# Layer 0 of a graph stack: seven block products in place of eight, and batch norm stepped block by block

## The chip, the cores and the metric

The kernel runs on one core of one Trainium2 chip, as one launch, all in float32. The metric is device time in microseconds (us). The times given for the kernel before are the median and the spread of three runs; the profile is of one further execution.

Names used below: PE is TensorE, ACT is ScalarE, DVE is VectorE, POOL is GpSimd, SP is SyncE, whose queue carries most transfers.

## What is computed

The reference is a stack of four graph layers over 128 graphs of 64 nodes and 256 features. Only layer 0 is touched by the change:

```python
h = jnp.maximum(_layernorm(x, axis=-1), 0.0)
agg = jnp.einsum('nm,bmd->bnd', A_hat, h)           # A_hat: normalized adjacency, 64 x 64
x1 = agg.reshape(-1, 256)
h = relu(_batchnorm(x1 @ W1.T + b1, g1, be1))       # W1: 512 x 256
out = _batchnorm(h @ W2.T + b2, g2, be2)            # W2: 256 x 512
x = x + out.reshape(128, 64, 256)
```

`_batchnorm` takes mean and variance over all 8192 rows, so nothing after the first product can be finished before the first product of every row is done, and the same holds for the second. Layers 1 to 3 (two graph convolutions with four LSTMs over windows, a masked attention, a four-head attention) follow; of them only the LSTM's bias, `bih + bhh`, is touched.

## The kernel before

The 8192 rows are cut into `NCH` = 16 chunks of `CH` = 512 rows. Results lie channels on partitions: one chunk of the first product is 4 blocks of 128 channels x 512 rows (`KH` = 4), its input 2 blocks (`KD` = 2).

**First stage, lines 452 to 521.** Per chunk: `norm0` (line 345) loads x on SP's queue, takes the layer norm's moments on DVE (lines 159, 160), the inverse root and the shift on POOL (lines 99, 100, 182, 183) and applies norm and relu in four tiles on ACT (line 187). `aggregate0` (line 349) multiplies by the adjacency in 64 small matmuls on PE (line 214) and copies the two PSUM banks, one by DVE (line 354), one by ACT (line 356). `product1` (line 358) is the product with W1: for each of four blocks two matmuls of 128x128 weights with 512 columns (line 369), an ACT copy that adds the bias (line 371), and DVE's batch-norm statistics (line 372). For chunks 1 to 15 only PE's order is that of the program (line 495); the order on the other engines is the planner's. On PE the order is aggregate of chunk c+1, product of chunk c.

**Batch norm, line 515.** `bn_params` (line 286) handles block after block: DVE aggregates the statistics (line 295), POOL takes the inverse root, three small DVE operations make scale and shift. `relu2` (line 375) applies them to chunks 0 and 1, and `product2` (line 521, matmuls on line 385) starts the second product on these two.

**Second stage, lines 591 to 659.** For chunks 2 to 14 the second product is already done by seven products of blocks (`Seven2`, line 398) in place of eight: input and weights are cut in two by two, four sums of input blocks (`differences`, line 304) and four sums of weights (`w2_sums`, made on POOL at line 508) are formed, and seven products (line 432) are combined through three PSUM banks X, Y and Z, with copies on ACT (line 439) and additions on DVE (line 443). All engines but SP follow the program's order. Chunk 15 comes last, by the plain product (lines 662 to 667), followed by the second batch norm and the first convolutions of layer 1 (the order list `START`).

What follows in the change uses the same scheme. The pool `l0b` has two buffers under the tag `h1`, `l0` two each under `h` and `agg` and three under `xt`; PSUM has eight banks. A tile that takes over a buffer waits for the last use of the tile that had it.

Of the kernel before, what the change touches and what calls it, by code (L numbers as in the profile page):

```python
# [8 lines left out]
F32 = mybir.dt.float32  # L9
AF = mybir.ActivationFunctionType  # L10
# [9 lines left out]
def kernel(  # L20
# [265 lines left out]
    def bn_params(stats, bn, pool, name, biased):  # L286


        n = stats.shape[1]
        mv = pool.tile([P, n, 2], F32, name=f"mv_{name}")  # L290
        sc = pool.tile([P, n], F32, name=f"sc_{name}")
        sh = pool.tile([P, n], F32, name=f"sh_{name}")
        for m in range(n):
            one = slice(m, m + 1)
            nc.vector.bn_aggr(mv[:, m, :], stats[:, m, :, :].rearrange("p c s -> p (c s)"))
            rsqrt(sc[:, one], mv[:, m, 1:2], EPS)
            if not biased:
                nc.vector.tensor_add(mv[:, m, 0:1], mv[:, m, 0:1], bn[:, 0, one])
            nc.vector.tensor_mul(sc[:, one], sc[:, one], bn[:, 1, one])
            nc.vector.tensor_mul(sh[:, one], mv[:, m, 0:1], sc[:, one])  # L300
            nc.vector.tensor_sub(sh[:, one], bn[:, 2, one], sh[:, one])
        return sc, sh
# [35 lines left out]

    def load0(c):
        xt = l0.tile([P, NJ, D], F32, tag="xt", name=f"xt_{c}", bufs=3)  # L340
        nc.sync.dma_start(xt, xr[c])
        hs[c] = l0.tile([P, NJ, D], F32, tag="h", name=f"h_{c}")
        return xt

    def norm0(c):
        xt = load0(c)
        ln_apply(hs[c], xt, *ln_stats(xt, f"a{c}"), f"a{c}", by_pool=True)

    def aggregate0(c):
        aggs[c] = l0.tile([P, KD, CH], F32, tag="agg", name=f"agg_{c}")  # L350
        dst = aggs[c].rearrange("p k (j e t) -> p e (k j) t", e=2, t=T)
        for e, ps in enumerate(aggregate(hs.pop(c), ahat_t, f"a{c}")):
            if e == 0:
                nc.vector.tensor_copy(dst[:, e], ps)
            else:
                nc.scalar.copy(dst[:, e], ps)

    def product1(c):
        agg = aggs.pop(c)
# [3 lines left out]
        for m in range(KH):  # L363
            if c == 0 and 2 * m == KH:
                aggregate0(1)
                ln_apply(hs[2], *third, "a2")
            ps = bank(f"z1_{c}_{m}")
            for k in range(KD):
                nc.tensor.matmul(ps, w1_sb[:, k, m * P : (m + 1) * P], agg[:, k, :],  # L369
                                 start=(k == 0), stop=(k == KD - 1))  # L370
            nc.scalar.activation(z1[c][m], ps, AF.Identity, bias=bn1_sb[:, 0, m : m + 1])
            nc.vector.bn_stats(st1[:, m, c, :], z1[c][m])
        z2[c], z1whole[c] = lo, (lo, hi)
# [15 lines left out]
    def result2(c, m, ps):  # L389
        nc.vector.tensor_scalar(z2[c][:, m, :], ps, bn2_sb[:, 0, m : m + 1], None, op0=OP.add)  # L390
# [7 lines left out]
    class Seven2:  # L398
# [39 lines left out]
        def copy(self, m, j, tag):  # L438
            nc.scalar.activation(self.part(m, j), self.banks[tag], AF.Identity,
                                 bias=bn2_sb[:, 0, m : m + 1])  # L440
# [6 lines left out]

    halves2 = [slice(0, CH // 2), slice(CH // 2, CH)]
# [3 lines left out]
    with tc.manual_schedule(engines={mybir.EngineType.PE, mybir.EngineType.DVE,  # L452
# [6 lines left out]
        xts = [l0.tile([P, NJ, D], F32, tag="xt", name=f"xt_{c}", bufs=3) for c in range(2)]  # L459
# [31 lines left out]
        xt = load0(2)  # L491
        third = xt, *ln_stats(xt, "a2")
        product1(0)
    tc.no_sync_barrier()
    with tc.manual_schedule(engines={mybir.EngineType.PE}):
# [5 lines left out]
        nc.gpsimd.dma_start(w2_sb, w2t.rearrange("(k p) f -> p k f", p=P))  # L501
        w2_sums = l0b.tile([P, 4, KH // 2, P], F32, name="w2_sums", bufs=1)
        a = w2_sb.rearrange("p (i k) (m f) -> p i m k f", i=2, m=KD)
        for dst, u, v, op in ((0, a[:, 0, 1], a[:, 1, 1], OP.add),
                              (1, w2_sums[:, 0], a[:, 0, 0], OP.subtract),
                              (2, a[:, 0, 0], a[:, 0, 1], OP.subtract),
                              (3, a[:, 1, 0], w2_sums[:, 1], OP.subtract)):
            nc.gpsimd.tensor_tensor(w2_sums[:, dst], u, v, op)
        for c in range(1, NCH):
            if c + 1 < NCH:  # L510
                aggregate0(c + 1)
            if c + 2 < NCH:
                norm0(c + 2)
            product1(c)
        sc1, sh1 = bn_params(st1, bn1_sb, w0, "bn1", True)
        for c in range(2):
            new_h1(c)
        for k in range(KH):
            for c in range(2):
                relu2(c, k)  # L520
# [140 lines left out]
    with tc.manual_schedule(engines={mybir.EngineType.PE}):  # L661
        c = NCH - 1
        banks = product2([c], False)
        for m in range(KD):
            result2(c, m, banks[c, m])
            stats2(c, m)
        sc2, sh2 = bn_params(st2, bn2_sb, const, "bn2", True)
# [19 lines left out]
    nc.vector.tensor_add(bias, bias, bias2)  # L687
# [503 lines left out]
    with tc.manual_schedule(engines={mybir.EngineType.PE, mybir.EngineType.DVE, mybir.EngineType.Pool,  # L1191
# [5 lines left out]
        for n, i in enumerate(START):  # L1197
            if n == 5:
                nc.vector.tensor_add(c2, c2_ps[:, :D], bg1_sb)
            for at, fill, name in ((6, 16, "d"), (9, 6, "e"), (10, 6, "f")):  # L1200
# [573 lines left out]
```

## Time and profile before

| what | value |
|---|---|
| median of three runs | 1912.3 us (1910.05 to 1912.66) |
| the profiled execution | 1910.73 us |
| its span, first to last instruction | 1908.6 us |
| PE, DVE, ACT, POOL busy in the span | 99%, 62%, 51%, 23% |
| granted TensorE clock | 1.0 |
| first product of chunks 1 to 15 | 23.4 to 144.4 us of the span |
| second product, all chunks | 144.4 to 246.8 us of the span |

How to read it: times in the views are from the start of the span. A row of the groups view has the line, the engine, the operation, output<-input, shape and count, then busy time and the mean of one instruction, then the idle time ahead of it and what ended it. Instructions of ACT, DVE and POOL that follow each other without a wait overlap a little: the distance from start to start is shorter than the duration. A float32 matmul shows as two records.

### The profile page before, as it was taken

Reading aid. Unit: us, or ns where it says so; the run is one execution under the profiler, and the core shown is the slowest. Engines: PE = TensorE matmul, PEld = TensorE weight load, DVE = VectorE, ACT = ScalarE, POOL = GpSimd, SP = SyncE. Lnnn points to the kernel's source line nnn. Section 1 sums busy time; section 2 is a strip of 40 time slices with the busy share of each in tenths; the row PEclk is TensorE's granted clock in tenths of the full one; section 3 lists DMA queues with packets and bytes.
Section 4 is the critical chain, followed back from the end, with each engine's and each line's share of the span. In section 5 each row is a group of like instructions: output and inputs, shape, how many; then the busy total and the mean of one; then the engine's idle time right before and its main releaser. Section 6 shows DMA issues by size and latency. Waiting matters only on the chain.

```text
span 1908.6 us, 38821 instructions
## 1 busy us (share of the span) xinstructions
PE 1887.0 (99%) x15137; PEld 1488.3 (78%) x15137; DVE 1190.7 (62%) x3070; ACT 979.5 (51%) x2184; POOL 444.6 (23%) x632
## 2 busy tenths in 40 slices
PE   8999999999999999999999999999999999999998
PEld 5446866886897898799689789879969967777776
DVE  6647844556557656655755764665555567777776
ACT  5657734455456455455544645545554544444453
POOL 4205711211211211121121121112112213232332
PEclk9999999999999999999999999999999999999999
DMA  4113653115424522531632452352144245444433
GB/s 137 60 39 138 223 195 108 49 78 188 132 84 161 182 84 77 189 103 70 215 117 84 161 182 84 103 186 100 54 155 127 92 133 156 134 150 139 144 112 112
DMA packets 110502, 240.39 MB, mean 126 GB/s; under 512 B 11376, under 2 KB 74352, under 8 KB 110320
## 3 DMA queue, kind: packets, MB, share of 16 engines
q1 hardware_dynamic: 109568, 236.57, 37.1%
q8 instruction: 120, 1.97, 0.4%
q0 software_dynamic: 320, 1.05, 0.2%
q14 instruction: 62, 0.51, 0.1%
q10 hardware_dynamic: 432, 0.30, 0.1%
HBM read 169.98 MB, written 67.90 MB: 125 GB/s over the span
## 4 chain that ended last, share of the span: by engine, by line
PE 93%; DVE 4%; ACT 1%; issue 1%; POOL 1%; DMA 0%; SPq 0%; DVEq 0%; ACTq 0%; POOLq 0%
PE x L990 23%; PE g L954 18%; PE z L990 11%; PE y L990 6%; PE v L1264 6%; PE z L369 5%; PE p_q L1271 3%; PE u L743 3%; PE v L729 3%; PE X L1460 3%; PE X L432 2%; PE Y L1460 1%; PE z L385 1%; PE Y L432 1%; PE agg_c L214 1%; PE o L1587 1%
## 5 line engine op out<-in xcount | busy, mean ns | idle before, releaser
L999 DVE TENSOR_TENSOR gates<-gates,x 128x128 f32<-128x128 f32 (+2 forms) x384 | 119.4, 322 | 333.1 <-PE x L990 327.7
L990 PE MATMUL x<-xd,wset 128*128 128x128 f32 (+2 forms) x1280 | 285.0, 310 | 0.1
L990 PE MATMUL x<-hd,wset 128*128 128x128 f32 (+2 forms) x1152 | 246.7, 303 | 0.0
L1048 POOL TENSOR_TENSOR gates<-gates 128x512 f32<-128x512 f32 (+2 forms) x48 | 75.0, 1562 | 647.9 <-ACT gates L882 647.9
L990 PEld LDWEIGHTS x<-xd,wset 128*128 128x128 f32 x1280 | 202.1, 190 | 16.9 <-DVE gates L999 3.1
L882 ACT ACTIVATE gates<-gates,bias 128x256 f32<-128x256 f32 (+4 forms) x384 | 170.4, 490 | 66.4 <-DVE gates L999 63.6
L990 PEld LDWEIGHTS x<-hd,wset 128*128 128x128 f32 x1152 | 185.1, 191 | 5.0
L933 ACT ACTIVATE gates<-g,bias 128x512 f32<-128x512 f32 (+2 forms) x240 | 138.2, 610 | 97.7 <-PE g L954 94.4
L954 PE MATMUL g<-hT,wset 128*128 128x256 f32 (+2 forms) x744 | 184.4, 405 | 1.1 <-DVE hT L893 1.1
L954 PEld LDWEIGHTS g<-hT,wset 128*128 128x128 f32 x744 | 140.5, 190 | 44.1 <-issue 8.8
L954 PE MATMUL g<-hT,wih 128*128 128x512 f32 x384 | 166.4, 592 | 0.0
L996 ACT COPY gates<-y 128x128 f32<-128x128 f32 (+2 forms) x192 | 54.2, 294 | 204.8 <-PE y L990 204.3
L990 PE MATMUL z<-hs,wset 128*128 128x128 f32 (+2 forms) x768 | 154.1, 303 | 0.0
L954 PEld LDWEIGHTS g<-hT,wih 128*128 128x128 f32 x384 | 72.3, 190 | 87.7 <-issue 83.0
L990 PEld LDWEIGHTS z<-hs,wset 128*128 128x128 f32 x768 | 119.8, 191 | 3.3
L369 PE MATMUL z<-agg,w_sb 128*128 128x512 f32 x256 | 114.1, 598 | 0.0
L939 DVE TENSOR_TENSOR cell<-gates 128x512 f32<-128x512 f32 (+2 forms) x80 | 50.5, 650 | 101.6 <-ACT gates L933 101.5
L999 DVE TENSOR_TENSOR gates<-gates,z 128x128 f32<-128x128 f32 (+2 forms) x384 | 104.6, 316 | 0.2
L996 ACT COPY gates<-x 128x128 f32<-128x128 f32 (+2 forms) x192 | 56.5, 296 | 93.7 <-PE x L990 93.0
L882 ACT ACTIVATE gates<-x,bias 128x128 f32<-128x128 f32 (+2 forms) x192 | 74.8, 390 | 50.9 <-PE x L990 48.1
L990 PE MATMUL z<-hT,wset 128*128 128x128 f32 (+1 forms) x512 | 96.9, 301 | 0.0
L369 PEld LDWEIGHTS z<-agg,w_sb 128*128 128x128 f32 x256 | 47.3, 190 | 54.6 <-issue 51.4
(271 smaller groups left out, 3827.0 us busy)
## 6 DMA issues: line engine op xcount, KB each, us to landing
wset<-wfar SPq DMA_DIRECT2D x96, 960.0 KB, 6.4
hT<-far_h SPq DMA_DIRECT2D x124, 128.0 KB, 2.9
far_h<-hm SPq DMA_DIRECT2D x16, 512.0 KB, 3.0
far_n<-xs SPq DMA_DIRECT2D x16, 512.0 KB, 6.9
xs<-far_n SPq DMA_DIRECT2D x64, 128.0 KB, 3.1
far_x<-xs SPq DMA_DIRECT2D x16, 512.0 KB, 3.0
x<-far_x SPq DMA_DIRECT2D x64, 128.0 KB, 3.2
xt<-in_x_dram SPq DMA_DIRECT2D x15, 512.0 KB, 4.0
```

The source lines that it names most:

```text
L369: nc.tensor.matmul(ps, w1_sb[:, k, m * P : (m + 1) * P], agg[:, k, :], start=(k == 0), stop=(k == KD - 1))
L432: nc.tensor.matmul(self.banks[tag], w, right[:, k, :], start=first and not k, stop=True, skip_group_check=True)
L729: nc.tensor.matmul(banks[m], wg0_sb[:, k, m * P : (m + 1) * P], agg[:, k, :], start=(k == 0), stop=(k == KD - 1))
L882: nc.scalar.activation(gate(q, c, part), src, AF.Tanh if q == 2 else AF.Sigmoid, bias=bs[:, q * KD + c : q * KD + c + 1])
L933: nc.scalar.activation(columns_of(gate(q, c)), natural(banks[q, c][:, :n].rearrange("p (w b) -> p w b", b=nb)), AF.Tanh if q == 2 else AF. ...
L954: nc.tensor.matmul(banks[q, c][:, :n].rearrange("p (w b) -> p w b", b=nb)[:, w, :], block(q, c, k), hv[:, k, w.start * p : (w.stop - 1) * ...
L990: nc.tensor.matmul(folded(self.psum(kind)), wsets[p, self.q][:, BLOCKS[kind][i], :], (ox[self.s] if part == "x" else oh)[kind], start=firs ...
L996: nc.scalar.copy(gate(self.q, kind // 5, halves[kind // 5]), self.psum(kind))
L999: nc.vector.tensor_add(gate(self.q, *dst), gate(self.q, *a), self.psum(kind))
L1048: nc.gpsimd.tensor_mul(gates[:, 0, :, :n], gates[:, 0, :, :n], gates[:, 2, :, :n])
L1264: nc.tensor.matmul(ps[:, i, :], hT[:, k, j, :], w[:, k, first : first + D], start=(k == 0), stop=(k == KD - 1))
L1460: nc.tensor.matmul(st[c, tag][:, i * CH // 2 : (i + 1) * CH // 2].rearrange("p (a n) -> p a n", n=P), w, st[c, "o7"][kind], start=first an ...
```

## The change

The first product of chunks 2 to 14 is done by seven block products (`Seven1`). The input chunk is cut in two blocks of channels times two halves of 256 rows; the sums of input blocks are formed on POOL per chunk (`differences`, 4 operations of 128x256), those of weights once (`w1_sums`, 4 operations). Each product is two matmul pairs of 256 columns into the halves of a bank. Products 7 and 4 of a chunk are done during the next chunk's turn. The addition of Z to block (0, 0) is done on POOL (`c11`), from an SBUF copy of Z made by ACT; the other two additions are on DVE. The four engines PE, DVE, ACT and POOL now follow a written order in this stage. Both PSUM banks of the aggregate are copied by ACT there. `w2_sums` moves from the stage's head into turns 7 to 10.

Biases of the two products are no longer added to the results; `bn_steps` adds the bias to the mean and gives it back in the shift, in two more small DVE operations per block. `bn_steps` is a generator: for the first batch norm its two halves for each block, and the relus of chunks 0 and 1, stand between the blocks of chunk 15. For the second, DVE takes chunk 15's statistics from PSUM, and ACT copies the result. `bias + bias2` for the LSTM is added a little later, at the fifth step of `START`.

```diff
-    def bn_params(stats, bn, pool, name, biased):
...
             one = slice(m, m + 1)
             nc.vector.bn_aggr(mv[:, m, :], stats[:, m, :, :].rearrange("p c s -> p (c s)"))
             rsqrt(sc[:, one], mv[:, m, 1:2], EPS)
+            yield
             if not biased:
                 nc.vector.tensor_add(mv[:, m, 0:1], mv[:, m, 0:1], bn[:, 0, one])
             nc.vector.tensor_mul(sc[:, one], sc[:, one], bn[:, 1, one])
             nc.vector.tensor_mul(sh[:, one], mv[:, m, 0:1], sc[:, one])
             nc.vector.tensor_sub(sh[:, one], bn[:, 2, one], sh[:, one])
-        return sc, sh
+            if not biased:
+                nc.vector.scalar_tensor_tensor(sh[:, one], bn[:, 0, one], sc[:, one], sh[:, one],
+                                               op0=OP.mult, op1=OP.add)
+            yield sc, sh
...
     def load0(c):
+            xts[c] = l0.tile([P, NJ, D], F32, tag="xt", name=f"xt_{c}", bufs=3)
+            nc.sync.dma_start(xts[c], xr[c])
...
+    def moments0(c):
+        return ln_moments(xts[c], f"a{c}", range(NJ)) if c < NCH else iter(())
+    def shift0(c, late):
+        for mv, rstd in late:
+            nmr = small.tile([P, NJ], F32, tag=f"ln_nmr{NJ}", name=f"nmr_a{c}")
+            nc.gpsimd.tensor_tensor(nmr, mv[:, :, 0], rstd, OP.mult)
+            nc.gpsimd.tensor_scalar(nmr, nmr, -1.0, None, op0=OP.mult)
+            shifts[c] = rstd, nmr
+    def apply0(c, *tiles):
...
+        for j in tiles:
+            nc.scalar.activation(hs[c][:, j, :], xts[c][:, j, :], AF.Relu, bias=nmr[:, j : j + 1],
+                                 scale=rstd[:, j : j + 1])
+    def aggregate0(c, by_both=True):
         aggs[c] = l0.tile([P, KD, CH], F32, tag="agg", name=f"agg_{c}")
         dst = aggs[c].rearrange("p k (j e t) -> p e (k j) t", e=2, t=T)
         for e, ps in enumerate(aggregate(hs.pop(c), ahat_t, f"a{c}")):
-            if e == 0:
+            if by_both and e == 0:
                 nc.vector.tensor_copy(dst[:, e], ps)
             else:
                 nc.scalar.copy(dst[:, e], ps)
-    def product1(c):
...
-            ps = bank(f"z1_{c}_{m}")
-            for k in range(KD):
-                nc.tensor.matmul(ps, w1_sb[:, k, m * P : (m + 1) * P], agg[:, k, :],
-                                 start=(k == 0), stop=(k == KD - 1))
-            nc.scalar.activation(z1[c][m], ps, AF.Identity, bias=bn1_sb[:, 0, m : m + 1])
+    def stats1(c, *ms):
+        for m in ms:
             nc.vector.bn_stats(st1[:, m, c, :], z1[c][m])
...
+    def block1(c, m, agg):
+        ps = bank(f"z1_{c}_{m}")
+        for k in range(KD):
+            nc.tensor.matmul(ps, w1_sb[:, k, m * P : (m + 1) * P], agg[:, k, :], start=(k == 0),
+                             stop=(k == KD - 1))
+        nc.scalar.copy(z1[c][m], ps)
+    class Seven1:
...
+        def __init__(self, c):
+            self.c, self.banks = c, {}
+            agg = aggs.pop(c)
+            b = {(k, j): agg[:, k, halves2[j]] for k in range(KD) for j in range(2)}
+            t = l0b.tile([P, KH, CH], F32, tag="h1", name=f"t1_{c}").rearrange("p k n -> p (k n)")
+            n = CH // 2
+            self.z = t[:, 4 * n : 6 * n]
+            t = [t[:, i * n : (i + 1) * n] for i in range(4)]
+            self.sums = differences(nc.gpsimd, t, b[0, 0], b[0, 1], b[1, 0], b[1, 1])
+            self.at = {1: b[0, 0], 2: b[1, 0], 3: b[1, 1], 4: t[3], 5: t[0], 6: t[1], 7: t[2]}
+        def product(self, kind, tag):
+            first = tag not in self.banks
+            if first:
+                self.banks[tag] = bank(f"{tag}1_{self.c}")
+            for i in range(2):
+                if kind in (1, 2, 4):
+                    m, k = {1: (0, 0), 2: (0, 1), 4: (1, 1)}[kind]
+                    w = w1_sb[:, k, (2 * m + i) * P : (2 * m + i + 1) * P]
+                else:
+                    w = w1_sums[:, {5: 0, 6: 1, 7: 2, 3: 3}[kind], i * P : (i + 1) * P]
+                nc.tensor.matmul(self.banks[tag][:, i * CH // 2 : (i + 1) * CH // 2], w, self.at[kind],
+                                 start=first and not i, stop=True, skip_group_check=True)
...
+        def copy(self, m, j, tag):
+            nc.scalar.copy(self.part(m, j), self.ps(tag))
+        def add(self, m, j, tag):
+            nc.vector.tensor_add(self.part(m, j), self.part(m, j), self.ps(tag))
+        def c11(self):
+            nc.gpsimd.tensor_tensor(self.part(0, 0), self.part(0, 0),
+                                    self.z.rearrange("p (i n) -> p i n", i=2), OP.add)
...
     def result2(c, m, ps):
-        nc.vector.tensor_scalar(z2[c][:, m, :], ps, bn2_sb[:, 0, m : m + 1], None, op0=OP.add)
+        nc.vector.tensor_copy(z2[c][:, m, :], ps)
...
         def copy(self, m, j, tag):
-            nc.scalar.activation(self.part(m, j), self.banks[tag], AF.Identity,
-                                 bias=bn2_sb[:, 0, m : m + 1])
+            nc.scalar.copy(self.part(m, j), self.banks[tag])
...
         l0b, close_l0b = pool("l0b", 2, "right")
         w2_sb = l0b.tile([P, KH, D], F32, name="w2_sb", bufs=1)
         nc.gpsimd.dma_start(w2_sb, w2t.rearrange("(k p) f -> p k f", p=P))
+        w1_sums = l0.tile([P, 4, D], F32, name="w1_sums", bufs=1)
         w2_sums = l0b.tile([P, 4, KH // 2, P], F32, name="w2_sums", bufs=1)
-        a = w2_sb.rearrange("p (i k) (m f) -> p i m k f", i=2, m=KD)
-        for dst, u, v, op in ((0, a[:, 0, 1], a[:, 1, 1], OP.add),
-                              (1, w2_sums[:, 0], a[:, 0, 0], OP.subtract),
...
-            nc.gpsimd.tensor_tensor(w2_sums[:, dst], u, v, op)
-        for c in range(1, NCH):
-            if c + 1 < NCH:
-                aggregate0(c + 1)
-            if c + 2 < NCH:
-                norm0(c + 2)
-            product1(c)
-        sc1, sh1 = bn_params(st1, bn1_sb, w0, "bn1", True)
-        for c in range(2):
-            new_h1(c)
-        for k in range(KH):
-            for c in range(2):
-                relu2(c, k)
+    def sums_of(dst, a):
+        return [lambda d=d, u=u, v=v, op=op: nc.gpsimd.tensor_tensor(dst[:, d], u, v, op)
+                for d, u, v, op in ((0, a[:, 0, 1], a[:, 1, 1], OP.add),
+                                    (1, dst[:, 0], a[:, 0, 0], OP.subtract),
+                                    (2, a[:, 0, 0], a[:, 0, 1], OP.subtract),
+                                    (3, a[:, 1, 0], dst[:, 1], OP.subtract))]
...
+    with tc.manual_schedule(engines={mybir.EngineType.PE, mybir.EngineType.DVE,
+                                     mybir.EngineType.Activation, mybir.EngineType.Pool}):
+        load0(3)
+        load0(4)
+        aggregate0(2)
+        late = moments0(3)
+        for _ in range(NJ):
+            next(late)
+        shift0(3, late)
+        for f in sums_of(w1_sums, w1_sb.rearrange("p k (m f) -> p k m f", m=2)):
+            f()
+        late = moments0(4)
+        next(late)
+        sevens = {2: Seven1(2)}
+        new_z1(1)
+        agg = aggs.pop(1)
+        load0(5)
+        for m in range(KH):
+            block1(1, m, agg)
+            if m < NJ - 1:
+                next(late)
+                apply0(3, *((0, 1), (2,), (3,))[m])
+            if m == NJ - 2:
+                shift0(4, late)
+            stats1(1, m)
+        for f in sevens[2].sums:
+            f()
+        more = sums_of(w2_sums, w2_sb.rearrange("p (i k) (m f) -> p i m k f", i=2, m=KD))
+        for c in range(2, NCH - 1):
+            a, z = sevens[c], sevens.get(c - 1)
+            new_z1(c)
+            load0(c + 4)
+            aggregate0(c + 1, False)
+            b = sevens[c + 1] = Seven1(c + 1) if c + 1 < NCH - 1 else None
+            late = moments0(c + 3)
+            a.product(2, "Z")
+            nc.scalar.copy(a.z, a.banks["Z"])
+            next(late, None)
+            next(late, None)
+            if z:
+                z.product(7, "X")
+                z.add(1, 1, "X")
+            if b:
+                for f in b.sums:
+                    f()
+            a.product(1, "X")
+            a.copy(0, 0, "X")
+            apply0(c + 2, 0)
+            a.c11()
+            if z:
+                stats1(c - 1, 0, 1)
+            a.product(5, "Y")
+            a.copy(1, 1, "Y")
+            apply0(c + 2, 1)
+            next(late, None)
+            next(late, None)
+            if z:
+                z.product(4, "X")
+                z.copy(1, 0, "X")
+            apply0(c + 2, 2)
+            shift0(c + 3, late)
+            if c > 6 and more:
+                more.pop(0)()
+            if z:
+                stats1(c - 1, 2, 3)
+            a.product(6, "X")
+            a.copy(0, 1, "X")
+            apply0(c + 2, 3)
+            a.product(3, "Y")
+            a.add(0, 1, "Y")
+        c = NCH - 1
+        new_z1(c)
+        agg = aggs.pop(c)
+        for m in range(KH):
+            if not m:
+                a.product(7, "X")
+                a.add(1, 1, "X")
+                stats1(c - 1, 0, 1)
+            if m == 1:
+                a.product(4, "X")
+                a.copy(1, 0, "X")
+                stats1(c - 1, 2, 3)
+            block1(c, m, agg)
+            stats1(c, m)
+            if not m:
+                steps1 = bn_steps(st1, bn1_sb, w0, "bn1", False)
+            else:
+                sc1, sh1 = next(steps1)
+                if m == 1:
+                    for i in range(2):
+                        new_h1(i)
+                for i in range(2):
+                    relu2(i, m - 1)
+            next(steps1)
+        sc1, sh1 = next(steps1)
+        for i in range(2):
+            relu2(i, m)
...
         banks = product2([0, 1], True)
...
         c = NCH - 1
         banks = product2([c], False)
         for m in range(KD):
-            result2(c, m, banks[c, m])
-            stats2(c, m)
-        sc2, sh2 = bn_params(st2, bn2_sb, const, "bn2", True)
+            nc.vector.bn_stats(st2[:, m, c, :], banks[c, m])
+            nc.scalar.copy(z2[c][:, m, :], banks[c, m])
+        *_, (sc2, sh2) = bn_steps(st2, bn2_sb, const, "bn2", False)
         c2_ps = weight_products()
...
-    nc.vector.tensor_add(bias, bias, bias2)
...
         for n, i in enumerate(START):
             if n == 5:
                 nc.vector.tensor_add(c2, c2_ps[:, :D], bg1_sb)
+                nc.vector.tensor_add(bias, bias, bias2)
```

## The prediction

> **What bounds the kernel now.** I read the page's busy shares first, then the chain that ended last, then the busy times of the stage that the change rewrites.
>
> ```profile
> PE 1887.0 (99%) x15137; PEld 1488.3 (78%) x15137; DVE 1190.7 (62%) x3070; ACT 979.5 (51%) x2184; POOL 444.6 (23%) x632
> ```
>
> PE is the bound over the whole span. The chain of waits, in order of time, shows the first stage (first two lines: one chunk) and a product of the second stage:
>
> ```profile
> 40.88 7.06 PE z L369 x16
> 47.95 1.09 PE agg_a L214 x64
> ...
> 186.10 1.73 PE X L432 x8
> ```
>
> A chunk costs PE 7.06 + 1.09 = 8.15 us in the first stage, and nothing else is on the chain. The stretch that holds chunks 2 to 14 (columns: length, then busy time of PE, PEld, DVE, ACT, POOL):
>
> ```profile
> 30.57:137.30 106.73, 106.42 (x1040) 52.22 (x1041) 60.83 (x153) 67.66 (x118) 20.52 (x48) 1.00 0.20 64
> ```
>
> PE has 0.3 us idle here, ACT 39, DVE 46, POOL 86. So less PE work pays directly, until one of the three is in the way.
>
> **What PE saves.** Two products of four records take 1.73 us in the chain, one 0.8635. Seven take 6.04 us where the plain product takes 7.06; with the aggregate a chunk needs 7.13. That is 1.02 us x 13 = 13.3 us. With it goes the wait at the first aggregate of the loop: in PE's timeline chunk 3's aggregate takes 1.94 us and 0.22 ahead of it, against 1.16, since its relus were late; about 0.9. If PE never waited, it would be at the second product 14.1 us earlier.
>
> **What the helpers now do per chunk.** Start-to-start distances are taken from ACT's and POOL's timelines:
>
> ```profile
> 33.75 1.58 ACT L187 ACTIVATE h<-xt,nmr_a,rstd_a 128x256 f32<-128x256 f32 x3
> 35.23 0.57 ACT L356 COPY agg<-agg_a 128x512 f32<-128x512 f32 x1
> 35.74 0.60 ACT L187 ACTIVATE h<-xt,nmr_a,rstd_a 128x256 f32<-128x256 f32 x1
> ```
>
> ```profile
> 25.17 1.41 POOL L508 TENSOR_TENSOR w_sums<-w_sb 128x256 f32<-128x256 f32 x2 [3.67 <-DMA w_sb<-in_w2t_dram]
> ...
> 195.79 3.70 POOL L580 TENSOR_TENSOR ws<-ws 128x256 f32<-128x256 f32 x4
> ...
> 235.27 2.91 POOL L580 TENSOR_TENSOR ws<-ws 128x256 f32<-128x256 f32 x4 [3.18 <-DMA ws<-in_whh_t_dram]
> ```
>
> ACT: a relu tile every 0.49 us, a copy of 512 every 0.48 (0.57 to 0.59 alone). New per chunk: seven copies and four relus, 5.3 us of 7.13. DVE: four moment pairs at 0.53 (starts 16.20, 16.76 in its timeline), four statistics at 0.60, two PSUM additions at 0.60: 5.7. POOL: inverse root and shift 1.98 with gaps (starts 91.41 to 93.37), four sums, `c11`. Nearest rows for the sums: 0.70 each undisturbed (1.41 for two), 0.93 beside DVE (3.70 for four); for `c11`, 128x512: 1.27 (row L1048) to 1.78 (the slow instances of L309). The Trainium skill (SBUF — State Buffer, section "Who interferes with whom") says that a DVE instruction with at most one SBUF input does not hold GpSimd up. The 3.70 ran beside DVE's L310 and L311 (two SBUF inputs), the 2.91 beside statistics and PSUM additions, and the new stage has only the latter kinds. By the page and that row I take 2.88 for the sums and 1.35 for `c11`, gaps included; by the disturbed rows they would be 3.8 and 1.86. POOL: 6.2, in turns 7 to 10 another 0.72 for `w2_sums`.
>
> A rule against the change: the Trainium skill (GPSIMD Engine Reference, section "Performance versus the Vector engine") measures elementwise work on GpSimd at 1.96 times DVE's time. Our rows agree (1.27 against 0.69 for 128x512), but on DVE the five operations would add 4 x 0.35 + 0.6 = 2.0 to 5.7, a turn of at least 7.7. On POOL they fit under 7.13, so I cost them there.
>
> **Two rings of waits.** Counted from E, the end of a turn's aggregate on PE; PE to another engine 0.21 us, ACT to PE 0.15.
>
> ACT's ring: Z, product 7, product 1 end at E+2.59; from E+2.80 ACT's queue is copy, relu, copy, relu, copy, relu, copy, relu: 7 x about 0.485 + 0.59 = 3.98, so the last relu tile is done at E+6.78. Queued on PE behind it is the last quarter (0.27) of the next aggregate, so the next E is at E+7.20. PE alone would give 7.13: a wait of 0.07 per turn.
>
> POOL's ring: the sums of chunk c+1 take over the buffer of chunk c-1, last read by product 4, which ends at E+4.32. If the sums wait for it (the trace before has no such case; a bound is no wait at all), they run E+4.53 to 7.41, `c11` to 8.76, root and shift to 10.74. The first relu of the next turn waits for that shift, and all ACT copies are queued behind that relu: six starts of 0.49 and 0.48 and the last 0.59 make 3.50, then 0.15 + 0.27. The E after next is at E+14.69 where PE alone gives 14.27. I take this wait in full: turns of 7.20 and 7.49 in alternation, mean 7.35. On DVE the statistics of block 0 wait for `c11` of the turn before, done at E+1.6; DVE reaches them at E+2.4, so the moments queued behind are not held.
>
> **Start of the loop.** In turn 2 PE has five products and an aggregate, 5.41 us. DVE copies the aggregate of chunk 2 at 25.0 as before, then four moment pairs to 27.8; POOL's shift for chunk 3 comes at 29.9. ACT's relus for it now alternate with the copies of chunk 1: last tile done 32.94, the aggregate at 33.55 instead of 31.58. POOL makes `w1_sums` to 32.9 and chunk 4's shift to 34.9, then the sums of chunk 2: product 5 waits 0.62, product 6 0.54. The turn takes 8.53, from 30.49 to 39.02. Turns 3 and 4 (7.28, 7.88) still carry POOL's backlog; then ten turns are 5 x 14.69 = 73.46. PE ends turn 14 at 127.65; products 7 and 4 (1.73) and chunk 15's plain product (7.06) bring it to 136.44, against 144.37: **7.9 us earlier**.
>
> **The rest.** *First batch norm:* today PE goes through without a gap:
>
> ```profile
> 133.64 10.89 PE L369 MATMUL z<-agg,w_sb 128*128 128x512 f32 x25
> 144.37 13.90 PE L385 MATMUL z<-h,w_sb 128*128 128x512 f32 x32
> ```
>
> so stepping it has nothing to gain there. In the written order chunk 15's third copy is queued on ACT behind the relus of block 0. Aggregate 0.6, root 1.0, five small operations at 0.2, then a relu of 0.8 make the relu of blocks 1 and 2 ready about 0.35 after PE wants it, twice: +0.7 (bounds 0 and 1.5). *Second stage:* PE loses about 1.9 us at its head, since DVE is late with additions; four plain copies at 0.60 for 0.66 (rows L354, L390) give -0.25. ACT's copies there get shorter (0.37, row L996, for 0.47), which PE does not wait for. *Second batch norm:* for block 1, result and statistics (0.74 + 0.69) shrink to statistics alone, and two small operations of 0.2 are added, so the scale is ready about 1.1 us earlier. But PE has weight products until 251.55 and starts the transposes at 252.02; at most 0.5 is open, and ACT's queue order may keep it: -0.3. The bias sum (0.19, row L687) moves ahead of a DVE step that others wait for: +0.1. `w2_sums` and the loads of x on SP's queue are moved past nothing that PE needs: loads land in 4.0 us, a turn is 7. Sum: -7.9 + 0.7 - 0.25 - 0.3 + 0.1 = **-7.65**. Against the profiled execution's 1910.7 that is 1903.1; the runs' median is 1.6 above it, so 1912.3 - 7.65 = **1904.6**.
>
> **Rivals.**
> *PE stays the bound.* No wait for the old buffer, or shorter ACT distances: all turns 7.13, the start smooth. 14.1 + 0.4: 1897.8. For it: no engine is asked for over 7.0 of 7.13. Against it: the relus' ring is already at 7.20. Chance 0.17.
> *ACT's queue is the bound.* If an operation that reads PSUM right after a wait does not overlap its neighbour (distance 0.57), ACT's ring is 7.8, and about 3.3 us remain: 1909. For it: PE releases most of these copies only shortly before. Chance 0.16.
> *Slower: POOL's ring.* At the disturbed prices, 3.8 and 1.86, two turns take 16.2, one 8.1, almost today's 8.15, and with turn 2 at 9.2 PE comes to the second product 2.2 us late; with the rest, 1914.7. It decides from about 5.4 us for sums and `c11` together (I take 4.2). Against it: DVE has no two-SBUF-input work in the stage. Chance 0.05.
>
> **How the numbers follow.** The forecast has 0.62 and by itself spans 1901 (no buffer wait, free boundary) to 1908 (POOL's sums at 0.84). A measurement of this kernel can tell about 0.2%, 3.8 us, from no change. Below 1908.5: all of the forecast, PE's case and half of ACT's, 0.87; within 0.2% the rest of ACT's and a little of POOL's, 0.09; slower 0.04. The range runs from PE's case to ACT's: 1897.5 to 1909.
>
> **What would show it.** PE at the second product at 136 to 137 us of the span; turns of 7.2 and 7.5 in alternation, with PE's wait on the last quarter of the aggregate, released by ACT's relu, and ACT's on POOL's shift; POOL idle until product 4 ends; three or more us lost in turn 2; sums near 0.72. Turns of 7.13 throughout, or POOL's sums starting right after the aggregate's copies, would prove the buffer wait wrong; a sum at 0.9 or an ACT distance of 0.57 would prove the prices wrong.

## The result, and the profile after

The changed kernel takes 1904.8 us (median of four runs, 1904.19 to 1904.91). Beside it the kernel before took 1912.48 (four runs, 1910.05 to 1912.7); the ratio is 0.9962, 95% interval 0.9945 to 0.9979. Over all runs of this study the medians of before lie between 1910.95 and 1912.48, so the gain is 6 to 8 us by the medians. The two profiled executions, both at a granted clock of 1.000, differ by less: 1910.73 against 1904.91 us, spans 1908.6 and 1903.0. The 43 runs of before whose clock is on record point the same way: their median is 1910.4 at a granted clock of 1.0 (3 runs), 1911.2 at 0.999 (31) and 1912.5 at 0.998 (9), while the changed kernel had 1.0 in three of its four and 0.999 in one. Whether the change itself has a part in the clock was not tried. What follows traces the 5.6 us by which the spans differ.

The page's busy shares, as read before:

```profile
PE 1879.9 (99%) x15293; PEld 1520.8 (80%) x15293; DVE 1201.7 (63%) x3093; ACT 980.6 (52%) x2212; POOL 499.7 (26%) x701
```

PE is still the bound and is 7.1 us less busy. The chain of waits shows the first products of a turn of the loop, and a plain product of the second stage without an aggregate beside it:

```profile
68.67 1.12 PE agg_a L214 x64
69.79 1.06 PE Z L426 x4
70.85 1.73 PE X L426 x8
72.58 0.86 PE Y L426 x4
...
233.08 6.87 PE z L455 x16
```

The products take 0.86 each (X is two here), but the one behind the aggregate takes 1.06. PE's timeline, which goes by the starts, has the same 0.2 in two places: 0.97 from the start of Z to the next product, and 0.95 for the last product ahead of an aggregate. (The aggregate is 32 matmuls, which show as 64 records.) The busy times of three stretches (columns: length, then PE, PEld, DVE, ACT, POOL, then granted clock, DMA share and GB/s): loop until the second product, second product until layer 1's first transpose, from there to the LSTM's first product.

```profile
30.24:136.82 106.58, 104.85 (x1212) 85.44 (x1213) 76.55 (x180) 77.44 (x149) 79.39 (x125) 1.00 0.22 66
136.82:245.02 108.20, 106.34 (x450) 83.20 (x448) 84.45 (x152) 66.77 (x129) 64.08 (x70) 1.00 0.56 200
245.02:272.74 27.72, 23.87 (x284) 16.92 (x285) 14.44 (x36) 10.09 (x17) 3.77 (x8) 1.00 0.42 175
```

The same points of before are 30.79, 144.37, 252.02 and 278.65, so:

| stretch | before, us | after, us | difference |
|---|---|---|---|
| to chunk 3's aggregate | 30.79 | 30.24 | -0.55 |
| to the second product | 113.58 | 106.58 | -7.00 |
| to layer 1's first transpose | 107.65 | 108.20 | +0.55 |
| to the LSTM's first product | 26.63 | 27.72 | +1.09 |
| to the end | 1629.95 | 1630.26 | +0.31 |

The first and the last line lie within what differs from profile to profile: chunk 3's aggregate starts at 30.02 to 30.96 in the changed kernel and its variants below, and the last stretch takes 1628.3 to 1630.3 over all profiles.

PE's timeline, with the aggregates of three turns, product 4 of two, and the last quarter of an earlier aggregate, which shows its wait (start, duration):

```profile
47.06 0.46 PE L214 MATMUL agg_a<-ahat_t,h 64*64 64x64 f32 x16 [0.30 <-ACT h L370]
...
58.35 1.03 PE L426 MATMUL X<-t,w_sb 128*128 128x256 f32 x4
...
61.04 1.39 PE L214 MATMUL agg_a<-ahat_t,h 64*64 64x64 f32 x64
...
65.92 1.03 PE L426 MATMUL X<-t,w_sb 128*128 128x256 f32 x4
...
68.60 1.19 PE L214 MATMUL agg_a<-ahat_t,h 64*64 64x64 f32 x64
...
75.96 1.39 PE L214 MATMUL agg_a<-ahat_t,h 64*64 64x64 f32 x64
```

Turns of 7.54 to 7.56 and of 7.36 alternate, up to the last (113.33, 120.69). In the long ones, here the first and the third, the aggregate is 0.2 longer, since its last quarter waits for ACT's last relu, as at 47.06. POOL's timeline says what held the relus up:

```profile
59.53 0.73 POOL L313 TENSOR_TENSOR t<-agg 128x256 f32<-128x256 f32 x1 [1.17 <-ACT z1b L436]
...
65.48 0.24 POOL L360 TENSOR_SCALAR nmr_a<-nmr_a 128x4 f32<-128x4 f32 x1
...
67.09 0.73 POOL L313 TENSOR_TENSOR t<-agg 128x256 f32<-128x256 f32 x1 [1.38 <-PE X L426]
...
69.97 1.28 POOL L442 TENSOR_TENSOR z1a<-z1a,t 128x512 f32<-128x512 f32 x1
...
73.04 0.24 POOL L360 TENSOR_SCALAR nmr_a<-nmr_a 128x4 f32<-128x4 f32 x1
```

and ACT's timeline goes on from POOL's two shifts (a copy of product 1, then the first relu):

```profile
65.25 0.58 ACT L436 COPY z1a<-X 128x512 f32<-128x512 f32 x1 [1.09 <-PE X L426]
65.75 0.60 ACT L370 ACTIVATE h<-xt,nmr_a,rstd_a 128x256 f32<-128x256 f32 x1
...
72.61 0.58 ACT L436 COPY z1a<-X 128x512 f32<-128x512 f32 x1 [1.09 <-PE X L426]
73.32 0.60 ACT L370 ACTIVATE h<-xt,nmr_a,rstd_a 128x256 f32<-128x256 f32 x1
```

POOL stands idle for 1.17 and 1.38 us, although the input of its sums has been in SBUF since the aggregate's copies. The two rows name different releasers, but both times the sums start 1.17 to 1.18 after the start of product 4, the last reader of the old buffer. Then sums, `c11`, root and shift follow each other. From the start of the sums to the relu it is 6.22 and 6.23 us; I had costed 2.88 + 1.35 + 1.98 = 6.21. In one turn of the pair the shift ends just in time: the relu at 65.75 starts 0.50 after the copy ahead of it, the queue's own distance. In the other it ends at 73.28, the relu starts 0.71 after the copy, and all of ACT's queue behind it is 0.2 later. The aggregate at 75.96 waits for that.

### The profile page after: what moved, and what is told of

It is laid out like the page before. It is cut to its first block, busy times and chain, and to the rows that moved or that the text cites. A ratio compares the mean times of both kernels' runs of the same rounds, so it can differ in the third digit from the quotient of the medians.

```text
span 1903.0 us, 39287 instructions
## 1 busy us (share of the span) xinstructions
PE 1879.9 (99%) x15293; PEld 1520.8 (80%) x15293; DVE 1201.7 (63%) x3093; ACT 980.6 (52%) x2212; POOL 499.7 (26%) x701
## 3 DMA queue, kind: packets, MB, share of 16 engines
q8 instruction: 121, 1.98, 0.4%
## 4 chain that ended last, share of the span: by engine, by line
PE 90%; DVE 5%; ACT 2%; issue 1%; POOL 1%; DMA 1%; SPq 0%; DVEq 0%; ACTq 0%
PE x L1159 23%; PE g L1123 18%; PE z L1159 11%; PE y L1159 6%; PE v L1434 5%; PE u L912 3%; PE v L898 3%; PE p_q L1441 3%; PE X L1630 3%; PE X L426 2%; PE X L502 2%; PE Y L1630 1%; PE Y L426 1%; PE agg_c L214 1%; PE o L1757 1%
## 5 line engine op out<-in xcount | busy, mean ns | idle before, releaser
L1159 PE MATMUL x<-hs,wset 128*128 128x128 f32 (+2 forms) x384 | 85.0, 303 | 0.0
L1228 ACT ACTIVATE gates<-cell 128x256 f32<-128x256 f32 (+2 forms) x144 | 55.3, 384 | 51.5 <-DVE cell L1227 51.0
```

Source lines behind the costliest of these rows:

```text
L1159: nc.tensor.matmul(folded(self.psum(kind)), wsets[p, self.q][:, BLOCKS[kind][i], :], (ox[self.s] if part == "x" else oh)[kind], start=firs ...
```

## The experiments

The theory to be tested: PE's own turn is about 7.33, not 7.13, because the change between the aggregate's 64x64 tiles and the products' 128x128 tiles costs PE some 0.2 us per turn, and the ring through POOL (wait for the old buffer's last reader, sums, shift, relus) makes every second turn longer. Rivals: the wait is POOL's own work and no buffer is involved; the gain lies in the parts without the bias; the 1.09 us at the LSTM is the work of the second batch norm.

**Is it the buffer? A first attempt, misbuilt.** The two buffers of input sums are made once and kept, so that each quarter waits for its own last reader and not for that of the whole tile.

```diff
+            if len(kept) < 2:
+                kept.append(l0b.tile([P, KH, CH], F32, tag="h1", name=f"t1_{c}"))
+            t = kept[c % 2].rearrange("p k n -> p (k n)")
```

> The changed kernel, with the two buffers of the input sums kept as two tiles for all chunks, so that each of POOL's four sums waits only for the last reader of its own quarter (only the fourth then waits for product 4). Buffer-wait theory: POOL's shift comes about 2.1 us earlier in the turn, the longer turns (7.56 in the changed kernel) fall to the shorter 7.36, six times 0.2: PE at the second product about 1.2 us earlier, 135.6 instead of 136.8, total near 1903.6. Rival (ACT's ring alone sets the long turns): alternation stays, 136.8, 1904.8. Rival of my sum on record (PE alone could do a turn in 7.13 and ACT's ring sets 7.20): turns fall to 7.20, PE there at 133.9.

Measured: 1916.26 us (ratio to before 1.0027, 1.0015 to 1.004), turns of 8.23. The sums stand in the program ahead of product 4, which reads the fourth quarter: on kept buffers product 4 of chunk c-1 reads the sum of chunk c+1 instead, so this kernel computes that product from other data, and waits for it. PE's timeline:

```profile
64.36 1.13 PE L430 MATMUL X<-t,w_sb 128*128 128x256 f32 x4 [0.63 <-POOL t L316]
```

It tells nothing of the theory. It only shows what a wait of PE on POOL in every turn costs: with product 4 waiting 0.63 us for a sum, the turn is longer than the old 8.15.

**The same, with the fourth sum behind product 4.** In the written order the fourth sum of chunk c+1 now follows product 4 of chunk c-1.

```diff
...
+            t = kept[c % 2].rearrange("p k n -> p (k n)")
...
-                for f in b.sums:
+                for f in b.sums[:2]:
                     f()
...
                 z.copy(1, 0, "X")
+            if b:
+                b.sums[2]()
```

> The changed kernel, with the two buffers of the input sums kept as two tiles for all chunks, and the fourth sum (the only one whose place product 4 still reads) moved behind product 4 and behind the addition of Z in POOL's queue. POOL can then make three sums right after the aggregate's copies. Buffer-wait theory: the shift is done before the next turn's relus ask for it, every turn falls to PE's own time, and that is 7.33 (1.09 + 0.97 + 5 x 0.8635 + 0.95, the first and last product of a turn as the changed kernel's trace has them), so 1.5 us less over the loop: 13 turns and the start from 30.2 end about 135.3, total 1903.3. Rival (ACT's own ring holds the long turns): the alternation 7.36, 7.56 stays, total 1904.8. Rival by my sum on record (PE could do 7.13): turns 7.20, total 1902.

Measured: 1903.59 (1903.55 to 1903.98), ratio to before 0.996 (0.9946 to 0.9973). From chunk 3's aggregate to the second product 105.40 us for 106.58. PE's and POOL's timelines:

```profile
60.74 1.17 PE L214 MATMUL agg_a<-ahat_t,h 64*64 64x64 f32 x64
...
68.08 1.17 PE L214 MATMUL agg_a<-ahat_t,h 64*64 64x64 f32 x64
...
75.42 1.17 PE L214 MATMUL agg_a<-ahat_t,h 64*64 64x64 f32 x64
```

```profile
63.17 0.73 POOL L313 TENSOR_TENSOR t<-agg 128x256 f32<-128x256 f32 x1 [1.11 <-ACT agg L380]
...
65.40 1.27 POOL L446 TENSOR_TENSOR z1a<-z1a,t 128x512 f32<-128x512 f32 x1
66.63 0.72 POOL L316 TENSOR_TENSOR t<-agg,t 128x256 f32<-128x256 f32 x1
```

The sums now start when ACT has copied the aggregate, as the theory of the buffer wait said, and all turns behind the loop's first three are 7.34 to 7.35. POOL does the same work per turn as before, so the old wait was the buffer's. That is also the end of the 7.13. A turn without a wait at the aggregate, as the run with the sums on DVE (below) has it, is made of 1.09 for the aggregate, 0.97 for Z, five products of 0.8635 and 0.95 for the last: 7.33 of PE's own.

**How tight is POOL's ring?** One more POOL addition of 128x256 per turn, behind `c11`; its result is not used.

```diff
+        extra = l0b.tile([P, D], F32, name="extra", bufs=1)
...
             a.c11()
+            nc.gpsimd.tensor_tensor(extra, w1_sums[:, 0], w1_sums[:, 1], OP.add)
```

> The changed kernel, with one more 128x256 addition on POOL per turn behind the addition of Z (0.70 us, its result unused). POOL's ring theory: two turns grow by the 0.70 of one turn, since the ring closes every second turn: 14.92 to about 15.6 per pair, 6 pairs, PE at the second product about 3.5 to 4.5 us later. Rival (PE bound, POOL has slack): no more than 0.3 us later. Rival (POOL serial, one turn per ring): 0.70 per turn, 8 to 9 us later.

Measured (one run): 1909.12 us, and 110.79 us from chunk 3's aggregate to the second product, 4.2 more. PE's timeline:

```profile
55.14 1.17 PE L214 MATMUL agg_a<-ahat_t,h 64*64 64x64 f32 x64
62.74 0.93 PE L214 MATMUL agg_a<-ahat_t,h 64*64 64x64 f32 x48
64.12 0.46 PE L214 MATMUL agg_a<-ahat_t,h 64*64 64x64 f32 x16 [0.46 <-ACT h L370]
...
70.76 1.17 PE L214 MATMUL agg_a<-ahat_t,h 64*64 64x64 f32 x64
```

A pair of turns takes 15.62, 0.70 more than 14.92: one operation of about 0.7 us on POOL, whole, once per pair. That is the mark of a ring that closes once in two turns. POOL is busy for 12.94 us of the pair's 15.62 here; it is not full, it is in series.

**What does the switch of tiles cost PE?** The aggregate is cut in two halves, one ahead of product 2 and one behind it, so that PE changes tiles four times a turn and not twice. (`begin0`, `tiles` and `finish0` are `aggregate0` in parts; both copies come after the second half.)

```diff
-            aggregate0(c + 1, False)
+            ps, tiles = begin0(c + 1)
+            tiles(0, 1)
+            a.product(2, "Z")
+            tiles(2, 3)
+            finish0(c + 1, ps)
...
-            a.product(2, "Z")
```

> The changed kernel, with each chunk's aggregate in the seven-product loop cut in two: two tiles, product 2, two tiles. PE's work is the same, but it changes between 64x64 and 128x128 tiles twice as often. Switch theory: each turn from aggregate to product and back costs PE about 0.19 us beyond the steady price of a product (0.97 and 0.95 against 0.8635), so turns grow by about 0.2, near 7.55 to 7.75, 2 to 2.5 us over the loop. Rival (the longer first and last products come from waits on copies): turns unchanged or shorter, since the relus have more time.

Measured (one run): 1907.33. PE's timeline:

```profile
69.32 0.69 PE L382 MATMUL agg_a<-ahat_t,h 64*64 64x64 f32 x32
69.95 1.13 PE L447 MATMUL Z<-agg,w_sb 128*128 128x256 f32 x4
71.01 0.69 PE L382 MATMUL agg_a<-ahat_t,h 64*64 64x64 f32 x32
71.63 1.13 PE L447 MATMUL X<-t,w_sums 128*128 128x256 f32 x4
...
77.01 0.69 PE L382 MATMUL agg_a<-ahat_t,h 64*64 64x64 f32 x32
```

The turn is 7.69, which is 0.35 more than 7.34 for two more changes; from chunk 3's aggregate to the second product it is 109.10, 2.5 more than in the changed kernel. The halves together take 1.25 for 1.10 (0.63 and 0.62), and from Z to the second half it is now 1.06 for 0.97, from X to the product behind it 0.97 for 0.8635. ACT's last relu ends at 69.98, a full 1.03 ahead of the second half, so no copy or relu holds it up. So going from one kind of matmul to the other does cost PE time, somewhat more than the 0.2 expected. The two kinds differ in tile size and in columns (64 against 256), and which of these it is was not separated.

**The sums on DVE.**

```diff
-            self.sums = differences(nc.gpsimd, t, b[0, 0], b[0, 1], b[1, 0], b[1, 1])
+            self.sums = differences(nc.vector, t, b[0, 0], b[0, 1], b[1, 0], b[1, 1])
```

> The changed kernel, with the four input sums of each chunk on DVE instead of POOL. By my costing DVE then has at least 5.7 + 4 x 0.35 = 7.1 us per turn plus waits in its fixed order (the statistics stand behind sums that wait for product 4), so turns of 7.7 or more: PE at the second product 2 to 5 us later than in the changed kernel, total 1907 to 1910. Rival (the skill's factor of two decides, and taking slow sums off POOL shortens its ring): turns at 7.36 throughout, total 1903.6.

Measured: 1911.13 (ratio to before 0.9998, 0.9989 to 1.0007), turns of 8.55. The direction was right, the price too low: I had taken 7.1 us of DVE's work and about 0.6 of waits, and missed how much DVE's own ring adds. PE's and DVE's timelines:

```profile
85.22 1.13 PE L426 MATMUL X<-t,w_sb 128*128 128x256 f32 x4 [0.95 <-DVE z1b L439]
...
93.77 0.48 PE L426 MATMUL X<-t,w_sb 128*128 128x256 f32 x1 [0.95 <-DVE z1b L439]
```

```profile
84.52 0.65 DVE L439 TENSOR_TENSOR z1b<-z1b,X 128x512 f32<-128x512 f32 x1
86.49 0.42 DVE L313 TENSOR_TENSOR t<-agg 128x256 f32<-128x256 f32 x1 [1.32 <-PE X L426]
```

A sum takes 0.42 on DVE and 0.73 on POOL. But in DVE's queue the sums wait for product 4, and product 4 waits for bank X, which DVE's addition of product 7 must leave first: DVE idles 1.32 and PE 0.95, each turn. It is this order of DVE's queue that was tried; another order was not.

**The bias part alone.** The kernel before, with the biases out of the results, the second batch norm's statistics from PSUM and the LSTM's bias sum moved; the first product stays plain, and the first batch norm is not stepped.

```diff
-            nc.scalar.activation(z1[c][m], ps, AF.Identity, bias=bn1_sb[:, 0, m : m + 1])
+            nc.scalar.copy(z1[c][m], ps)
...
-        sc1, sh1 = bn_params(st1, bn1_sb, w0, "bn1", True)
+        sc1, sh1 = bn_params(st1, bn1_sb, w0, "bn1", False)
...
-            result2(c, m, banks[c, m])
-            stats2(c, m)
+            nc.vector.bn_stats(st2[:, m, c, :], banks[c, m])
+            nc.scalar.copy(z2[c][:, m, :], banks[c, m])
...
```

> The kernel before, with only the second part of the change: no bias added to the two products' results, bias given back through scale and shift, chunk 15's second statistics from PSUM, LSTM bias sum moved. The planner orders as before. My costing: between 0 and -0.5 us, total 1912. Rival (this part carries the gain, or a good share of it): 2 us or more faster.

Measured: 1910.69 (ratio to before 0.9997, 0.9988 to 1.0005). From chunk 3's aggregate to the second product it is 113.57 for 113.58, so the 7.00 us there come from the rest of the change: the seven products in their written order. (The order alone was not tried. Before, PE had 0.1 us idle in that stretch, and its first aggregate took 1.94 for 1.16, so with the same products an order had less than 1 us to win.) At the second stage's head PE has three waits for DVE (0.21, 0.55, 0.54), before two (0.34, 0.64) and a third product that started 0.18 late; from the second product to layer 1's first transpose it is 107.85 for 107.65. So this part holds 0.2 of the 0.55 lost there.

**The LSTM's first product.** In the changed kernel it starts late; PE's timeline and DVE's:

```profile
272.74 7.11 PE L1123 MATMUL g<-hT,wih 128*128 128x512 f32 x16 [0.83 <-issue]
```

```profile
271.95 0.69 DVE L918 TENSOR_TENSOR cv<-u,c 128x512 f32<-128x512 f32 x1 [0.98 <-PE u L912]
```

DVE's last bias addition reads a PSUM bank until 272.64. The kernel gives its eight PSUM banks out in turn, and the seven products take 13 fewer than the plain ones, one less per chunk: the LSTM's first bank would now be the one that DVE still reads. If so, taking five more banks anywhere ahead must remove the wait. The filler on PE at the kernel's start is spread over six banks in place of one, with the same number of matmuls:

```diff
-        keep_busy(34, "a")
+        for i, n in enumerate((6, 6, 6, 6, 5, 5)):
+            keep_busy(n, f"a{i}")
```

> The changed kernel, with the first run of 34 filler transposes at the head spread over six PSUM banks instead of one, so five more banks are taken from the ring of eight before the layer's end; no work is added. The seven products take five banks a chunk where six were taken, 13 fewer in all, so the ring's phase had moved by five of eight. Bank theory: PE's unexplained wait of 0.83 us (1.2 on its weight loads) ahead of the LSTM's first product at 271.8, where a bank still being read by DVE's last bias addition is handed on, disappears: total 0.8 to 1.2 us less, near 1903.8, by the trace. Rival (instruction fetch or another cause by position): the wait stays.

Measured: 1903.7 (1902.86 to 1903.82), ratio to before 0.996 (0.9946 to 0.9975), and PE's timeline without a wait:

```profile
272.54 7.03 PE L1124 MATMUL g<-hT,wih 128*128 128x512 f32 x16
```

It starts 26.73 after layer 1's first transpose (after: 27.72; before: 26.63), with all the work of the second batch norm in place. So the bank costs 0.99. The 0.1 that remain are also in the run with the bias part alone (26.74).

**The gains together, with one more.** The kept buffers and the six banks, and chunk 0's two results of the second product copied by ACT, not DVE, against the waits at the second stage's head.

```diff
-                    result2(0, m, banks[0, m])
+                    nc.scalar.copy(z2[0][:, m, :], banks[0, m])
```

> Everything that the traces pointed to, together: sums in quarters (as in the run before), the filler spread over six banks (as in the fourth run), and at the head of the second stage chunk 0's two result copies on ACT instead of DVE. Sum of the parts: -1.5 for the loop, -1.0 for the bank, and 0.5 to 1.2 of the 1.6 + 0.8 us that PE loses there to late additions of DVE: 1901.5 against 1904.8. Rival[...]: the third part gives nothing, 1902.3.

Measured: 1902.43 (1902.1 to 1903.85), ratio to before 0.9956 (0.9942 to 0.997). The waits at the head shrank, from three (0.46, 0.54, 0.55) to one of 0.34, so it was mostly DVE's two copies that had made the additions late. But a new wait came at the stage's end. PE's, POOL's and ACT's timelines:

```profile
228.21 1.13 PE L506 MATMUL Y<-z1b,w_sums 128*128 128x256 f32 x4 [1.61 <-ACT z1a L513]
```

```profile
223.64 2.90 POOL L757 TENSOR_TENSOR ws<-ws 128x256 f32<-128x256 f32 x4 [4.33 <-DMA ws<-in_whh_t_dram]
226.49 1.26 POOL L314 TENSOR_TENSOR t<-z1b,z1a 128x512 f32<-128x512 f32 x1
```

```profile
227.79 0.37 ACT L513 COPY z1a<-Y 128x256 f32<-128x256 f32 x1 [3.32 <-POOL t L314]
```

POOL's queue holds four sums of LSTM weights ahead of chunk 14's last input sum; they start when their load lands, so the sum is late, ACT's copy behind it, and PE needs the bank. From the second product to chunk 15's it took 96.58 us, against 96.09 after the change and 96.09 without the third edit (next run): that edit gained nothing. Whether ACT's extra copies make the load land late, or it varies, was not tried.

**The two gains alone.** The same without the third edit.

> The changed kernel with the two buffers for the input sums filled in two groups (the last sum behind c11), and with the start-up filler spread over six PSUM banks, but with chunk 0's two results on DVE as in the changed kernel. My theory: the two gains add. The turns are 7.34 each, PE comes to the second product near 135.4 us of the span (1.2 to 1.4 earlier than in the changed kernel), and the LSTM's first product starts 26.7 us after the aggregate of layer 1 without a wait (1.0 less), so about 1904.8 - 1.2 - 1.0 = 1902.6, the head of the second stage as in the changed kernel. Rival: the time won in the first stage is given back in the second, since POOL and ACT come to it with the same backlog (the third edit's version showed such a wait of 1.6 us at chunk 15): second product to aggregate 1 us longer than the changed kernel's 108.2, and 1903.5 or above.

Measured: 1902.59 (1901.88 to 1903.07), ratio to before 0.9947 (0.9934 to 0.9961). The windows view, same three stretches:

```profile
30.26:135.66 105.40, 103.74 (x1213) 84.86 (x1213) 76.56 (x180) 76.93 (x149) 79.75 (x125) 1.00 0.21 67
135.66:243.86 108.20, 106.34 (x450) 83.06 (x448) 83.90 (x152) 66.81 (x129) 63.44 (x70) 1.00 0.55 199
243.86:270.59 26.73, 23.70 (x284) 17.06 (x285) 13.75 (x35) 10.10 (x17) 3.78 (x8) 1.00 0.45 187
```

The gains add: 1.18 us in the first line and 0.99 in the third against the changed kernel, nothing given back in the second. This and the one with the third edit are the best of the study, 2.2 to 2.4 us below the changed kernel, and not to be told apart.

## Why the prediction was right, and where its terms were off

The forecast case happened: PE stays the bound, and POOL's ring adds a wait to every second turn. The mechanism is right. That 1904.6 stands against 1904.8 is luck in part. The sum of the terms was -7.65, and the spans differ by 5.6. For a profiled execution the forecast was 1903.1, and it took 1904.91. The medians agree because that of before lay 1.6 above its profile, and that of the changed kernel did not (1904.8 for 1904.91).

- **POOL's ring: right, in mechanism and price.** Sums 0.73 (predicted 0.70 to 0.72), `c11` 1.28, 6.22 to the relu for 6.21. The pair of turns came at 14.92 for 14.69. (The terms written down add to 14.66; 0.03 of the 14.69 is in none of them.) Most of the difference lies ahead of the sums, which start 4.73 after the aggregate's end for 4.53: Z is 0.10 longer from start to start, and the sums follow product 4 about 0.1 later than I took. The wait for the old buffer, of which the trace before had no case, was taken in full; the run with kept buffers shows it. The two rivals without it, or with it at disturbed prices, fell.
- **What PE saves: mis-sized.** "Seven take 6.04 us where the plain product takes 7.06." The 7.06 held the change from the aggregate's tiles, the 6.04 did not; the plain product without an aggregate beside it takes 6.87. Like for like it is 6.87 - 6.04 = 0.83 per chunk, 10.8 us for 13, not 13.3. For the same reason "PE alone" was 7.33 and not 7.13, and the rival in which PE stays the bound throughout was some 2.6 us too low. In the run with kept buffers all turns are at PE's own pace, and it is only 1.2 us better than the changed kernel.
- **ACT's ring: its distances held, its length did not.** Relu to copy to relu starts are 0.46 to 0.51 apart, so the rival with 0.57 fell. But the queue starts later behind the aggregate than I took, 2.89 for 2.80 (with kept buffers: aggregate done at 61.84, copy at 64.73), and the last relu ends 4.01 after that (68.74). With 0.15 and 0.27 that is 7.32 for 7.20. So ACT's ring is all but as long as PE's own turn of 7.33; by this sum less work on PE alone would have met it at once.
- **Start of the loop: right.** Turn 2 took 8.26 for 8.53, turns 3 and 4 together 15.19 for 15.16.
- **The loop as a whole: 0.4 us late, from misses of both signs.** PE came to the second product at 136.82 for 136.44. Ten turns took 74.46 us for 73.46. Against that, chunk 3's aggregate started 0.25 earlier, turn 2 was 0.27 shorter, and chunk 15 with the two late products took 8.67 for 8.79.
- **First batch norm: +0.7 did not come.** PE's timeline has no gap between chunk 15 and the second product, and the second product takes no longer than before but for 0.1:

```profile
131.67 5.31 PE L396 MATMUL z<-agg,w_sb 128*128 128x512 f32 x12
136.82 13.98 PE L455 MATMUL z<-h,w_sb 128*128 128x512 f32 x32
```

- **Second stage's head: wrong sign.** I took -0.25, and it came to +0.55. The waits for DVE's additions rose from two (0.98 us together) to three (1.55). The cheaper copies for chunk 0 did not shorten what PE waits for. The bias part alone accounts for 0.2; what makes the rest was not tried.
- **Second batch norm: nothing, for -0.3.** Layer 1's first transposes start with the same waits as before (0.31 and 0.21, released by ACT's L880): ACT's order keeps it, the case that I had named and not taken.
- **The LSTM's bias sum: +0.1, as predicted.** It shows once the bank's wait is away: 26.73 for 26.63.
- **Not foreseen: the LSTM's bank, +0.99.** I followed each moved instruction through the queues, but not the count of PSUM banks.

## What to carry to other kernels

Cost a change from two rows taken in the same surroundings: a product measured beside a switch of tile sizes (7.06) and one measured without it (6.87) are not comparable. When an operation is handed to an idle engine, follow the ring through it (buffer's last reader, its own work, what it releases) over as many turns as there are buffers; an engine that is 77 to 83% busy, as POOL was here (11.55 of 14.92 us, 12.94 of 15.62), can still set the pace, and splitting the reuse of a buffer by its parts can take it out. When the number of PSUM banks taken changes, look at who holds the bank of the next dense stage.

## What the hardware showed that was not expected

- Going between the aggregate's 64x64 matmuls and the products' 128x128 ones costs PE time: in the chain the product behind an aggregate takes 1.06 for 0.8635 us, and two more changes per turn cost 0.35 us (7.69 for 7.34).
- Four POOL sums of 128x256 beside DVE's statistics and PSUM additions stayed at 0.72 to 0.74 us each in all turns of the changed kernel. The LSTM's sums of the same shape, in the second stage of the changed kernel and its variants, took 2.89 to 4.34 us for four, that is the same price at best and 1.09 each at worst.
- A bank handed over late, five places off in a ring of eight, costs PE 0.99 us some 136 us after the stage that caused it.
